# A planned two-layer kernel: VectorE work recorded one instruction at a time, and a plan that weighs what waits behind a task

## The chip, the cores and the metric

The kernel runs on one core of a Trainium2 chip. A core has a matmul engine (TensorE, PE in the profile, with its weight loads as PEld), a vector engine (VectorE, DVE), an engine for activation functions (ScalarE, ACT), a general engine (GpSimd, POOL) and SyncE (SP), which issues most DMAs here. Each engine works through its own queue in order; semaphores tie the queues together. The metric is the device time of one execution, in microseconds (us). A profile is one execution taken with the hardware profiler.

## The reference, cut to what matters

An input of 16 x 256 tokens of 128 features goes through four stages, each with a residual and a normalisation without weights:

```python
    x = _layernorm(x + _L0_attn_ref(x, ...), axis=-1)   # 16 heads of 64, softmax over 256 keys
    x = _layernorm(x + _L0_ffn_ref(x, ...), axis=-1)    # token routed to one of 64 spline tiles
    x = _layernorm(x + _L1_attn_ref(x, ...), axis=-1)   # linear attention and a window of 65, gated
    x = _layernorm(x + _L1_ffn_ref(x, ...), axis=-1)    # causal attention, then 8 experts
```

The last one is the longest:

```python
        h = layernorm(x, ln_g, ln_b)
        q = l2norm((h @ Wq) per head) * q_scale
        k = l2norm((h @ Wk) per head) * k_scale
        logits = q @ k.T * QK_SCALE, masked to the causal half
        out = (softmax(logits) @ v) @ Wo
        h = layernorm(out, ln_g, ln_b)
        gate = softmax(h @ gate_w + gate_b)
        hid = gelu(h @ w1[e] + b1[e])
        moe = sum over e of gate[e] * (hid @ w2[e] + b2[e])
        return layernorm(moe, ln_g, ln_b)
```

All eight experts are computed for every token. Everything is float32.

## The kernel before, in words

**Tiling.** The 4,096 tokens form 8 groups (`NG`) of 512, four tiles (`NJ`, index `j`) of 128 tokens on partitions. Each group goes through five stages, functions `stage_a` (attention of layer 0), `stage_b` (routing to spline tiles), `stage_c` (linear and window attention), `stage_d` (causal attention) and `stage_e` (experts). A group's activations stay in one buffer `x` in SBUF; five groups have one at a time.

**Recording and planning.** The stages do not issue instructions. They call `W.add(engine, cost, function, r=, w=)`, which records a task: the engine that may run it (a letter; "VS" lets the planner choose VectorE or ScalarE), a cost in ns, the objects it reads and writes, and `at`, a due place on a common scale (group number plus stage number plus a fraction). `add` derives from reads and writes which tasks wait for which. Buffers are taken from classes of slots (`SLOTS`): a task that first touches a buffer needs a free slot.

`Plan.order` (L144) then builds the whole order at once. It keeps a clock per engine, and repeatedly takes, over all engines, the task that could start earliest, ties going to the smaller `at`. A start takes in the ends of its forerunners plus `LAG` of their engine (`OWN` if it is the same engine), the free slots, 1,300 ns (`SWITCH`) for a change of the ScalarE table, and 93 ns (`DRAIN`) for a change of matmul tile shape (`mode`). A gelu of the experts carries a `burst`: ScalarE, once it has begun a burst (two experts, eight gelus), runs nothing else until the burst is done. The resulting order is issued as it is; each engine's queue is fixed by it.

**Places that the change touches.**

- `pair` (L577) does one pair of heads of stages a and d: `scores` into a two-bank PSUM tile `s` (there are two such tiles), `top` (in d: add the causal mask L607, two maxima L612, a product L614; in a: one maximum L616), per head `weigh` on ScalarE (exp, L634), a reciprocal (L641), `norm` on POOL (L647), a transposition on PE (L662), a copy (L529 on ACT, L531 on DVE) and `values`.
- `layernorm` (L533): `stats` (four statistics L540 and four aggregates L542), `root` on POOL (L545, L549) and `scaled` (L553), each one task for all four tiles.
- `affine` (L922): gamma, beta and residual as three POOL operations over 512 columns (L927).
- `rsqrt` (L1146): one task of 12 small VectorE steps, each reading the one before, L1152 to L1160.
- Window attention in `stage_c` (L935): masked queries `qm` made on POOL (L1031), `top` (L1064, L1065), `divide` (L1109, L1110).
- `stage_e` (L1320): both weights of an expert in one slot `we` (two slots); `up` matmuls into gelu (L1346), `down` matmuls per tile `j`, and one task `gated` of four multiply-adds into `moe` (L1361); after the last expert `layernorm`, `affine`, `layernorm` and the output DMA (L1368).
- All matmuls through the helper `mm` have line L523.

Of the kernel before, what the change touches and what calls it, by code (L numbers as in the profile page):

```python
# [46 lines left out]
    ("ov", 256, 8),  # L47
    ("m", 64, 26),
    ("k1", 256, 4),
    ("b", 512, 2),  # L50
    ("sc", 288, 1),
    ("c", 512, 8),
    ("qm", 512, 2),
    ("pbC", 512, 2),
# [5 lines left out]
    ("e", 512, 1),  # L60
    ("hid", 512, 5),
    ("we", 1024, 2),
# [20 lines left out]

class Plan:

    LAG = {"P": 270.0, "V": 150.0, "S": 170.0, "G": 120.0, "Q": 0.0, "D": 0.0}
    OWN = 80.0
    SWITCH = 1300.0  # L90
    DRAIN = 93.0

# [8 lines left out]
    def add(self, eng, cost, fn, r=(), w=(), at=None, table=None, burst=None, mode="f", hold=()):  # L101
# [9 lines left out]
        for objs, writes in ((r, False), (w, True)):  # L111
            for o in objs:
                o, part = o if isinstance(o, tuple) else (o, None)
                if isinstance(o, Buf):
                    bufs[id(o)] = o
                for q, (writers, readers) in self.state.setdefault(id(o), {}).items():
                    if part is None or q is None or q == part:
                        before.update(writers)
                        if writes:
                            before.update(readers)  # L120
# [23 lines left out]
    def order(self):  # L144
        free = {e: 0.0 for e in "PVSGQD"}
# [17 lines left out]
        while done < len(self.tasks):  # L163
            best = None
            avail = {c: sorted(x for x in v if x is not None) for c, v in slots.items()}
            for e, ts in cand.items():
                pick = None
                for t in ts:
# [3 lines left out]
                    for x, end in t.ready.items():  # L172
                        start = max(start, end + (self.OWN if x == e else self.LAG[x]))
# [65 lines left out]
def kernel(ctx: ExitStack, tc: tile.TileContext, a: dict, out: bass.AP):  # L239
# [293 lines left out]
    def layernorm(o, z, name, after=()):  # L533

        mv, rs = W.buf("m", "mv" + name), W.buf("m", "rs" + name)

        def stats():
            st = mv()[:, 8 : 8 + NJ * 6].rearrange("p (j s) -> p j s", s=6)
            for j in range(NJ):
                nc.vector.bn_stats(st[:, j, :], z(J, d=D)[:, j, :])  # L540
            for j in range(NJ):
                nc.vector.bn_aggr(mv()[:, 2 * j : 2 * j + 2], st[:, j, :])  # L542

        def root():
            nc.gpsimd.tensor_scalar(  # L545
                rs()[:, NJ : 2 * NJ], mv()[:, 0 : 2 * NJ].rearrange("p (j s) -> p j s", s=2)[:, :, 1], EPS, 1.0,
                ALU.add, ALU.mult,
            )
            nc.gpsimd.tensor_tensor(out=rs()[:, 0:NJ], in0=rs()[:, NJ : 2 * NJ], in1=mhalf, op=ALU.pow)  # L549

        def scaled():
            for j in range(NJ):
                nc.vector.tensor_scalar(  # L553
                    o(J, d=D)[:, j, :], z(J, d=D)[:, j, :], mv()[:, 2 * j : 2 * j + 1], rs()[:, j : j + 1],
                    ALU.subtract, ALU.mult,
                )

        W.add("V", NJ * (195 + 70), stats, r=[z, *after], w=[mv])
        W.add("G", 1300, root, r=[mv], w=[rs])
        W.add("V", NJ * 257, scaled, r=[z, mv, rs], w=[o])  # L560

# [15 lines left out]
    def pair(pi, qT, kT, v, ov, causal, rq, un=0):  # L577
# [24 lines left out]
        def top():  # L602
            s = sps(S2, a=2)
            n = nmx(n=4, pattern="p (a b) -> p a b", a=2)
            if causal:
                diag = s[:, :, P : 3 * P].rearrange("p a (b k) -> p a b k", k=P)
                nc.vector.tensor_tensor(  # L607
                    out=diag, in0=diag, in1=cmask.unsqueeze(1).unsqueeze(1).to_broadcast([P, 2, 2, P]), op=ALU.add
                )
                for qc in range(2):  # L610
                    c0, nk = col[qc]
                    nc.vector.tensor_reduce(n[:, :, qc], s[:, :, c0 : c0 + nk], AX.X, ALU.max, negate=True)  # L612
                rqp = rq("p (b i m) -> p i m b", n=16, b=2, i=2)[:, pi, 2 * un : 2 * un + 2, :]
                nc.vector.tensor_tensor(out=n, in0=n, in1=rqp, op=ALU.mult)  # L614
            else:
                nc.vector.tensor_reduce(n, s.rearrange("p a (b k) -> p a b k", k=S), AX.X, ALU.max, negate=True)  # L616

        cost = 1790 if causal else dve(1024)
        W.add("V", cost, top, r=[rq] if causal else [], w=[sps, nmx])
# [207 lines left out]
    def stage_b(g):  # L827
# [82 lines left out]
        def add_up():  # L910
            for q, j in enumerate(order):
                V.scalar_tensor_tensor(
                    y(J, d=D)[:, j, :], pv()[:, q, 65:NPAR], mag()[:, q : q + 1], xx(J, d=D)[:, j, :], ALU.mult, ALU.add
                )

        W.add("V", 4 * 259, add_up, r=[pp, mag, xx], w=[y, end_b])
# [5 lines left out]
    def affine(y, gam, bet, xx):  # L922

        nJ = [P, NJ, D]
# [10 lines left out]
    def stage_c(g):  # L935
# [48 lines left out]
        for b in range(2):  # L984
# [24 lines left out]
            def divide(b=b, pn2=pn2, rden=rden):  # L1009
                r = rden()[:, :2]  # L1010
                V.tensor_scalar(r, pn2()[:, :, D], 1e-6, None, ALU.add)
                V.reciprocal(r, r)
                V.tensor_tensor(
                    out=lin(J, d=D)[:, 2 * b : 2 * b + 2, :], in0=pn2()[:, :, :D],
                    in1=r.unsqueeze(2).to_broadcast([P, 2, D]), op=ALU.mult,
                )

            W.add("V", 360 + dve(256), divide, r=[pn], w=[rden, (lin, b)])
# [3 lines left out]
            for i, (w0, w1_) in enumerate(win_of):  # L1022
# [39 lines left out]
                def top(sps=sps, nmx=nmx, nk=nk, t0=t0):  # L1062
                    s8 = sps("p (u k) -> p u k", u=8)[:, :, :nk]
                    V.tensor_tensor(out=s8, in0=s8, in1=band[:, :, t0 : t0 + nk], op=ALU.add)  # L1064
                    V.tensor_reduce(nmx()[:, :8], s8, AX.X, ALU.max, negate=True)  # L1065

                W.add("V", 130 + 2 * dve(8 * nk), top, w=[sps, nmx])
# [40 lines left out]
                def divide(po=po, rw=rw, c0=c0):  # L1108
                    V.reciprocal(rw()[:, :QC], po()[:, QC : 2 * QC])  # L1109
                    V.tensor_tensor(out=winT()[:, c0 : c0 + QC], in0=po()[:, :QC], in1=rw()[:, :QC], op=ALU.mult)  # L1110

                W.add("V", 700, divide, r=[po], w=[rw, (winT, (b, i))])
# [33 lines left out]
    def rsqrt(o, x, n, eps):  # L1146

        ve, y, u = W.buf("m", "ve"), W.buf("m", "y"), W.buf("m", "u")

        def go():  # L1150
            V = nc.vector
            V.tensor_scalar(ve(n=n), x(n=n), eps, None, ALU.add)  # L1152
            yi = y(n=n).bitcast(I32)
            V.tensor_scalar(yi, ve(n=n).bitcast(I32), 1, None, ALU.logical_shift_right)
            V.tensor_scalar(yi, yi, -1.0, float(0x5F3759DF), ALU.mult, ALU.add)
            for k in range(3):
                src, dst = (y, o) if k % 2 == 0 else (o, y)
                V.tensor_mul(u(n=n), src(n=n), src(n=n))
                V.scalar_tensor_tensor(u(n=n), u(n=n), -0.5, ve(n=n), ALU.mult, ALU.mult)
                V.scalar_tensor_tensor(dst(n=n), u(n=n), 1.5, src(n=n), ALU.add, ALU.mult)  # L1160

        W.add("V", 2465 + 12 * (n - 16), go, r=[x], w=[ve, y, u, o])

    def stage_d(g):
# [9 lines left out]
        def half(b, hf):  # L1174
# [13 lines left out]
            for u in range(2):  # L1188
# [12 lines left out]
                def keep(e, ps_q=ps_q, qT=qT, u=u):  # L1201
                    for i in range(2):
# [7 lines left out]
                W.add("VS", (782, 714), keep, r=[ps_q], w=[qT])  # L1210
# [109 lines left out]
    def stage_e(g):  # L1320
# [4 lines left out]
        n = NJ * NE  # L1325
        tg, gT, pb2, moe = W.buf("p", "tg"), W.buf("k1", "gT"), W.buf("p", "pb2"), W.buf("e", "moe")
# [3 lines left out]
        W.add("VS", (dve(512), scl(512)), lambda e: copy(e, moe(), pb2()), r=[pb2], w=[moe])  # L1330
        for e_ in range(NE):
            W.at = base + e_ / NE
            burst = (g, e_ // NBURST)
            we = W.buf("we", "we")

            def fetch(e_=e_, we=we):
                nc.sync.dma_start(out=we()[:, :512], in_=a["L1_ffn_w1"][e_])
                nc.sync.dma_start(out=we()[:, 512:].rearrange("p (c d) -> p c d", d=D), in_=a["L1_ffn_w2"][e_].rearrange("(c p) d -> p c d", p=P))

            W.add("Q", 5000, fetch, w=[we], at=W.at - 0.2)  # L1340
            pe_, hids = W.buf("p", "pe"), []
            for c in range(NFC):
                ph, hid = W.buf("p", "phE"), W.buf("hid", "hid")
                W.add("P", pe(512), lambda ph=ph, we=we, c=c: mm(ph(), we()[:, c * P : (c + 1) * P], h2()), r=[we, h2], w=[ph, chain_e], burst=burst, hold=[hid])
# [3 lines left out]
            for j in range(NJ):  # L1348
                def down(j=j, pe_=pe_, we=we, hids=hids):
                    for c in range(NFC):  # L1350
                        mm(
                            pe_()[:, j * P : (j + 1) * P], hids[c]()[:, j * P : (j + 1) * P], we()[:, 512 + c * D : 512 + (c + 1) * D],
# [3 lines left out]
                W.add("P", pe(P, count=NFC), down, r=[we] + hids, w=[(pe_, j)])  # L1356

            def gated(e_=e_, pe_=pe_):
                for j in range(NJ):
# [3 lines left out]
            W.add("V", 4 * 259, gated, r=[pe_, gate], w=[moe])  # L1363
        W.at = base + 1.0
        layernorm(moe, moe, "E1")
        affine(moe, lngb, lnbb, xx)
        layernorm(xx, moe, "E2")
        W.add("Q", 2500, lambda: nc.sync.dma_start(out=y_out[g], in_=xx(J, d=D)), r=[xx])  # L1368
# [47 lines left out]
```

## Time and profile before

| | |
|---|---|
| median of 3 runs | 2226.43 us (2225.33 to 2226.8) |
| the profiled execution's own time | 2226.4 us |
| its span, first to last instruction | 2224.7 us |
| mean granted TensorE clock | 0.986 |
| last matmul ends | 2208.76 us |
| ScalarE table loads | 59, 1283 ns each |

In a row of groups stand: line, engine, operation, tile written and tiles read (buffer numbers left out), shapes, count | busy time of all, mean ns of one | idle time of the engine just before them and what ended it. A row of waits names the waiting engine and line, what it waited for, and total, times and longest in us. "Busy" of an engine is the union of its instructions; ends of matmuls are modelled.

| engine | busy us | share of the span |
|---|---|---|
| PEld | 1563.7 | 70% |
| DVE | 1663.4 | 75% |
| ACT | 1308.8 | 59% |
| POOL | 784.0 | 35% |

### The profile page before, as it was taken

The numbers are of one execution on the slowest core, as the hardware profiler recorded it, in microseconds if no ns is written. First come the engines' busy times: TensorE is split into PE (matmuls) and PEld (weight loads), VectorE is DVE, ScalarE is ACT, GpSimd is POOL, SyncE is SP. The second block draws the span as 40 slices with busy tenths as digits, with TensorE's granted clock in tenths as the row PEclk, the third lists the DMA queues.
The fourth block names the chain that finished last, engine by engine and source line by source line (L and its number), as shares of the span: only waits on it lengthen the run. The fifth ranks groups of instructions, "written<-read, shape, count | busy, mean of one in ns | idle before, by whom it ended". The sixth has DMA issues, their size and how long they took to land.

```text
span 2224.7 us, 49747 instructions
## 1 busy us (share of the span) xinstructions
PE 2099.0 (94%) x18506; PEld 1563.7 (70%) x18506; DVE 1663.4 (75%) x4784; ACT 1308.8 (59%) x3817; POOL 784.0 (35%) x1413
## 2 busy tenths in 40 slices
PE   8999999999999998999999999999899989989987
PEld 6777777767767766776777767777667667766655
DVE  5788899886688965788757895788856984784742
ACT  4566666764667643676647664666545755654632
POOL 3444362452143621435304360243502530431311
PEclk9999999999999999999999999999999999999998
DMA  5100000000100001000010001100011001101101
GB/s 141 30 1 2 2 1 2 2 2 26 48 15 2 2 29 35 25 2 1 23 41 25 2 1 40 39 6 2 2 43 34 7 2 55 27 1 44 39 20 43
DMA packets 69490, 47.98 MB, mean 22 GB/s; under 512 B 12064, under 2 KB 59904, under 8 KB 69248
## 3 DMA queue, kind: packets, MB, share of 16 engines
q1 hardware_dynamic: 68672, 43.74, 7.3%
q8 instruction: 147, 2.41, 0.5%
q10 hardware_dynamic: 576, 1.05, 0.2%
q14 instruction: 95, 0.78, 0.1%
HBM read 41.89 MB, written 2.88 MB: 20 GB/s over the span
## 4 chain that ended last, share of the span: by engine, by line
PE 53%; DVE 20%; ACT 5%; POOL 2%; issue 2%; POOLq 0%; DVEq 0%; ACTq 0%
PE p L523 39%; PE s L523 6%; PE p L662 4%; DVE m L612 2%; ACT pb L634 2%; PE p L1082 2%; DVE s L607 2%; DVE m L540 1%; DVE m L616 1%; POOL pb L647 1%; DVE x L553 1%; DVE m L614 1%; PE p L1265 1%; DVE uq L1208 1%; DVE s L1064 1%
## 5 line engine op out<-in xcount | busy, mean ns | idle before, releaser
L647 POOL TENSOR_SCALAR pb<-pb,m 128x256 f32<-128x256 f32 (+1 forms) x1024 | 453.8, 460 | 766.9 <-DVE m L641 675.1
L1346 ACT ACTIVATE hid<-p,b 128x512 f32<-128x512 f32 x256 | 170.5, 688 | 304.7 <-PE p L523 290.4
L662 PE MATMUL p<-ident,pb 128*128 128x128 f32 x1792 | 290.0, 282 | 14.1 <-POOL pb L647 5.0
L634 ACT ACTIVATE pb<-s,m,m 128x128 f32<-128x128 f32 (+1 forms) x512 | 257.4, 522 | 61.5 <-DVE m L614 50.7
L634 ACT ACTIVATE pb<-s,m 128x256 f32<-128x256 f32 x512 | 238.8, 490 | 70.5 <-DVE m L616 59.4
L662 PEld LDWEIGHTS p<-ident,pb 128*128 128x128 f32 x1792 | 206.1, 142 | 102.0 <-POOL pb L647 46.8
L523 PE MATMUL p<-h,we 128*128 128x512 f32 x512 | 264.2, 617 | 9.5 <-ACT hid L1346 4.9
L523 PEld LDWEIGHTS p<-we,hid 128*128 128x128 f32 x2048 | 243.3, 194 | 29.9 <-issue 15.7
L523 PE MATMUL p<-we,hid 128*128 128x128 f32 x2048 | 252.8, 279 | 3.9 <-ACT hid L1346 2.1
L529 ACT COPY pt<-p 128x512 f32<-128x512 f32 (+1 forms) x316 | 168.6, 540 | 129.1 <-PE p L662 117.3
L1361 DVE SCALAR_TENSOR_TENSOR e<-p,m,e 128x128 f32<-128x128 f32 x256 | 71.9, 344 | 143.7 <-PE p L523 122.0
L616 DVE TENSOR_REDUCE m<-s 128x4 f32<-128x1024 f32 x128 | 154.7, 1217 | 15.7 <-PE s L523 14.5
L1255 POOL TENSOR_TENSOR kn<-kn,m 128x512 f32<-128x512 f32 x64 | 66.2, 1049 | 283.9 <-DVE m L1160 232.3
L1076 ACT ACTIVATE pbC<-s,m 128x96 f32<-128x96 f32 (+1 forms) x512 | 135.3, 382 | 33.8 <-DVE m L1065 29.3
L523 PE MATMUL s<-ua,ua 64*128 64x256 f32 x1024 | 139.4, 395 | 10.5 <-ACT pb L634 9.0
L523 PE MATMUL s<-ud,uq 64*128 64x128 f32 (+1 forms) x1024 | 118.0, 352 | 21.4 <-ACT pb L634 20.4
L523 PE MATMUL p<-pt,ua 128*64 128x256 f32 x1024 | 136.2, 388 | 1.7 <-ACT pt L529 1.3
L531 DVE COPY pt<-p 128x512 f32<-128x512 f32 (+1 forms) x196 | 120.9, 621 | 20.9 <-PE p L662 19.5
L612 DVE TENSOR_REDUCE m<-s 128x2 f32<-128x256 f32 (+1 forms) x256 | 130.8, 553 | 5.3
L523 PEld LDWEIGHTS p<-h,we 128*128 128x128 f32 x512 | 84.9, 193 | 64.4 <-issue 30.6
L1031 POOL TENSOR_TENSOR qm<-c,hm 128x512 f32<-128x512 f32 x64 | 68.1, 1070 | 153.4 <-PE s L523 132.8
L523 PEld LDWEIGHTS s<-ua,ua 64*128 64x128 f32 x1024 | 91.2, 187 | 39.5 <-ACT pb L634 14.3
(273 smaller groups left out, 4294.0 us busy)
## 6 DMA issues: line engine op xcount, KB each, us to landing
we<-in_L_ffn_w_dram SPq DMA_DIRECT2D x128, 256.0 KB, 2.8
x<-_attn_hidden_states_dram SPq DMA_DIRECT2D x8, 256.0 KB, 2.8
out_dram<-x SPq DMA_DIRECT2D x8, 256.0 KB, 2.3
dpad<-k SPq DMA_DIRECT2D x1, 768.0 KB, 10.3
wq<-in_L_attn_Wq_dram ACTq DMA_DIRECT2D x2, 256.0 KB
wkv<-in_L_attn_Wkv_dram ACTq DMA_DIRECT2D x2, 256.0 KB, 6.8
wkv<-in_L_attn_Wkv_dram SPq DMA_DIRECT2D x2, 256.0 KB, 5.6
wo<-in_L_attn_Wo_dram SPq DMA_DIRECT2D x1, 512.0 KB, 8.4
```

What stands on the lines that cost most here:

```text
L523: nc.tensor.matmul(o, lhsT=lhsT, rhs=rhs, start=start, stop=stop)
L529: nc.scalar.copy(o, i)
L531: nc.vector.tensor_copy(o, i)
L612: nc.vector.tensor_reduce(n[:, :, qc], s[:, :, c0 : c0 + nk], AX.X, ALU.max, negate=True)
L616: nc.vector.tensor_reduce(n, s.rearrange("p a (b k) -> p a b k", k=S), AX.X, ALU.max, negate=True)
L634: act(pb()[:, c0 : c0 + nk], s[:, par, c0 : c0 + nk], AF.Exp, bias=nmx()[:, 2 * par + qc : 2 * par + qc + 1], accum_out=sums()[:, 2 * par ...
L647: eng.tensor_scalar(pb()[:, c0 : c0 + nk], pb()[:, c0 : c0 + nk], sums()[:, 2 * par + qc : 2 * par + qc + 1], 1.0, ALU.mult, ALU.mult,)
L662: nc.tensor.transpose(tps()[:, at * P : (at + 1) * P], pb()[:, c0 + kc * P : c0 + (kc + 1) * P], ident)
L1031: (V if e == "V" else G).tensor_tensor(out=qm("p (h q) -> p h q", q=QC), in0=qw()[:, c0 : c0 + QC].unsqueeze(1).to_broadcast(nq), in1=hm8. ...
L1076: act(pb("p (u k) -> p u k", u=4)[:, u, :nk], s8[:, hp, :nk], AF.Exp, bias=nmx()[:, hp : hp + 1])
L1346: W.add("S", 571, lambda ph=ph, hid=hid, ec=ec: act(hid(), ph(), AF.Gelu_apprx_tanh, bias=b1[:, ec : ec + 1]), r=[ph], w=[hid], table="gel ...
L1361: V.scalar_tensor_tensor(m, pe_()[:, j * D : (j + 1) * D], gate()[:, j * NE + e_ : j * NE + e_ + 1], m, ALU.mult, ALU.add)
```

## The change

Tasks on VectorE that held several instructions become one task per instruction: `layernorm`'s statistics, aggregates and scaling, `top` and `divide` of the attentions, `add_up` in stage b, `rsqrt`, `gated`. Parts of an object can now be named by a kind and a number (`("j", j)`), and `overlap` decides whether two parts conflict: parts of different kinds do, different parts of the same kind do not.

The planner gets other lags, an `OWN` per engine, and a new outer loop: `rest` of a task is its cost plus the longest chain of tasks behind it; the due place becomes `at - rest / weight`; ten weights are planned, and the order whose planned end is earliest is issued. The weight that results here is 4e4.

An expert's weights lie in two slots of their own classes (`w1`, `w2`), loaded by two tasks. `begun` lets the expert matmuls start only when `moe` has been set. The last group's norms, affine and output run tile by tile, with the affine on VectorE and its result kept in `moe`. Slot counts change.

```diff
-    ("ov", 256, 8),
-    ("m", 64, 26),
-    ("k1", 256, 4),
+    ("ov", 256, 7),
+    ("m", 64, 30),
+    ("k1", 256, 5),
...
-    ("c", 512, 8),
-    ("qm", 512, 2),
-    ("pbC", 512, 2),
+    ("c", 512, 7),
+    ("qm", 512, 1),
+    ("pbC", 512, 3),
...
-    ("e", 512, 1),
-    ("hid", 512, 5),
-    ("we", 1024, 2),
+    ("e", 512, 2),
+    ("hid", 512, 6),
+    ("w1", 512, 2),
+    ("w2", 512, 2),
...
-    LAG = {"P": 270.0, "V": 150.0, "S": 170.0, "G": 120.0, "Q": 0.0, "D": 0.0}
-    OWN = 80.0
+    LAG = {"P": 265.0, "V": 178.0, "S": 200.0, "G": 60.0, "Q": 0.0, "D": 0.0}
+    OWN = {"P": 0.0, "V": 130.0, "S": 80.0, "G": 80.0, "Q": 0.0, "D": 0.0}
+    RESTS = (1e5, 8e4, 6e4, 5e4, 4e4, 3e4, 2.5e4, 2e4, 1.5e4, 1e4)
...
-                    if part is None or q is None or q == part:
+                    if overlap(q, part):
...
     def order(self):
+        rest = {}
+        for t in reversed(self.tasks):
+            rest[t.seq] = min(t.cost) + max([self.LAG[t.eng[0]] + rest[n.seq] for n in t.then], default=0.0)
...
+        def again(weight):
+            for t, t.wait, at in first[0]:
+                t.ready, t.end, t.at = {}, None, at - rest[t.seq] / weight
...
+        for weight in self.RESTS:
+            line = again(weight)
+            if line is not None:
+                ends.append((max(end for _, _, _, end in line), weight))
+        return again(min(ends)[1])
...
-    def layernorm(o, z, name, after=()):
+    def layernorm(o, z, name, after=(), js=range(NJ), own=False):
+        if own:
+            for j in js:
+                layernorm(o, z, name, after, [j])
+            return
...
-        W.add("V", NJ * (195 + 70), stats, r=[z, *after], w=[mv])
-        W.add("G", 1300, root, r=[mv], w=[rs])
-        W.add("V", NJ * 257, scaled, r=[z, mv, rs], w=[o])
+        for j in js:
+            W.add("V", 195, lambda j=j: nc.vector.bn_stats(st(j), z(J, d=D)[:, j, :]), r=[*zs, *after], w=[(mv, ("j", j))])
+        for j in js:
+            W.add("V", 70, lambda j=j: nc.vector.bn_aggr(mv()[:, 2 * j : 2 * j + 2], st(j)), w=[(mv, ("j", j))])
...
+        W.add("G", 1300 if len(js) == NJ else 800, root, r=[mv], w=[rs])
...
-        W.add("V", 2465 + 12 * (n - 16), go, r=[x], w=[ve, y, u, o])
+        each = lambda fn, r, w: W.add("V", 60 + n, fn, r=r, w=w)
+        each(lambda: V.tensor_scalar(ve(n=n), x(n=n), eps, None, ALU.add), [x], [ve])
...
-            we = W.buf("we", "we")
+            w1, w2 = W.buf("w1", "w1"), W.buf("w2", "w2")
+            W.add("Q", 2500, lambda e_=e_, w1=w1: nc.sync.dma_start(out=w1(), in_=a["L1_ffn_w1"][e_]), w=[w1], at=W.at - 0.2)
...
-            W.add("V", 4 * 259, gated, r=[pe_, gate], w=[moe])
+                W.add("V", 259, gated, r=[pe_, gate], w=[(moe, ("j", j))])
...
-        layernorm(moe, moe, "E1")
-        affine(moe, lngb, lnbb, xx)
-        layernorm(xx, moe, "E2")
-        W.add("Q", 2500, lambda: nc.sync.dma_start(out=y_out[g], in_=xx(J, d=D)), r=[xx])
+        last = g == NG - 1
+        layernorm(moe, moe, "E1", own=last)
+        affine(moe, lngb, lnbb, xx, own=last)
+        if last:
+            layernorm(moe, moe, "E2", own=True)
+            for j in range(NJ):
+                W.add("Q", 2500, lambda j=j: nc.sync.dma_start(out=y_out[g][:, j, :], in_=moe(J, d=D)[:, j, :]), r=[(moe, ("j", j))])
+        else:
+            layernorm(xx, moe, "E2")
+            W.add("Q", 2500, lambda: nc.sync.dma_start(out=y_out[g], in_=xx(J, d=D)), r=[xx])
```

## The prediction

> **What bounds the kernel.** I read the busy shares first, then the waits of TensorE, then stretches of the span, then single instructions.
>
> ```profile
> span 2224.7 us, 49747 instructions
> ...
> PE 2099.0 (94%) x18506; PEld 1563.7 (70%) x18506; DVE 1663.4 (75%) x4784; ACT 1308.8 (59%) x3817; POOL 784.0 (35%) x1413
> ```
>
> TensorE is busy for 94% of the span; nothing in the change removes a matmul. A busy PE is still not a full one. At the steady start-to-start times of the trace (one pass over 512 columns 430 ns, 256 columns 216, 128 columns 111, halves and quarters where tiles run side by side), all matmul passes add up to about 1,880 us. So 2224.7 - 1880 = 345 us is loss, in five parts: the tail behind the last matmul, 15.9 (it ends at 2208.8); visible idle of PE before that, 109.8; changes of tile shape (below), 81; a granted clock of 0.986, about 29; and the rest, about 105, short delays hidden under the modelled length of the matmul before.
>
> Of the 109.8, added up over all rows of the waits by the engine waited for, ACT ended 47.8, DVE 40.6, POOL 15.8, a DMA at the start 5.6. So 104 us stand in 2,100 us of work, mostly about 1 us at a time. The largest row (total, times, longest) is scores that wait for a PSUM bank which exp still reads:
>
> ```profile
> PE s L523 <- ACT pb L634: 30.5, 27, 4.4
> ```
>
> Where they stand, by stretches (length, then busy time per engine):
>
> ```profile
> 400.00:520.00 120.00, 116.94 (x1097) 87.67 (x1096) 105.30 (x297) 81.13 (x268) 61.73 (x111) 1.00 0.01 2
> ...
> 2000.00:2080.00 80.00, 77.50 (x476) 54.36 (x477) 37.49 (x108) 36.41 (x75) 8.71 (x18) 0.98 0.16 47
> 2080.00:2150.00 70.00, 59.51 (x412) 41.07 (x411) 51.34 (x167) 43.17 (x135) 31.23 (x61) 0.93 0.05 12
> ```
>
> In the first, attention of several groups overlaps: PE idles 3 us, but DVE is 88% busy, a second bound. In the second, experts stand amid other work and DVE is only half used. In the third the last group's attention (stage d) stands alone: 10.5 us of 70 idle.
>
> **The change, part by part.** It is mostly another order of the same work, so I counted in the instruction orders of both kernels.
>
> *VectorE in single instructions.* Neighbours on DVE where the second reads what the first wrote fall from 1,079 to 308 (norm statistics, scaling and gated sums, which share only the tile's name, left out). What one costs:
>
> ```profile
> L542 DVE BATCH_NORM_AGGREGATE m<-m 128x2 f32<-128x6 f32 x288 | 26.2, 155 | 0.0
> ...
> L1158 DVE TENSOR_TENSOR m<-m 128x32 f32<-128x32 f32 x96 | 20.4, 213 | 3.4
> L1047 DVE TENSOR_TENSOR vm<-p,bvw 96x32 f32<-96x32 f32 x128 | 15.1, 177 | 2.2 <-PE p L523 2.2
> ```
>
> Busy time over count against mean length: L542 takes 155 ns each but only 91 of engine time, L1047 177 and 118; independent instructions overlap. L1158, each reading its forerunner, takes 213 of 213. In the timeline the rsqrt's steps start 225 ns apart, L1047's 97. So a dependent neighbour costs 0.13 us, and 771 fewer save 100 us of DVE. The Trainium skill says otherwise ("VectorE: DVE Perf Modes", Rules for kernel authors): chained operations drain in any case, one should lower their count, not the semaphores. The count here rises (4,784 to 4,899), so by the rule DVE loses a little. The row decides: 91 against 155 is overlap. Against the 100 stand 90 copies that move from ACT to DVE, at 0.6 us about 54. DVE falls to about 1,615.
>
> *Table loads.* 59 become 36; gelus run in 10 groups (six of 32) instead of 23.
>
> ```profile
> L1346 ACT ACT_TABLE_LOAD x23 | 29.5, 1283 | 0.4
> ```
>
> 23 x 1.283 = 29.5 us off ACT; "ScalarE: Activation LUTs" (What ACT_TABLE_LOAD costs) adds a drain, 2.66 us a switch, 61 in all. In the trace the next activation starts 1.29 us after the load, so 29.5 stands. With the copies gone ACT falls by about 80, to 1,230. Neither saving is the span's: both engines are off the bound. They count only through PE's waits.
>
> *PE's waits.* For each matmul group that reads another engine's result, I set the PE work between it and the group that feeds that engine against the length of the chain in between (start-to-start: an exp of two tiles 0.90, a 512-column copy 0.60). Groups with too little PE work in between: score transpositions 42 of 512 before, 24 after; values 41 and 21 of 256; down projections 26 and 16 of 256. The summed shortfall falls by 24%. Queueing on ACT and DVE is not in it, and improves too. Of 104 us I take 24%: **-25**; bounds 0 and -52. The 105 of hidden delays come of the same closeness, but the trace doesn't name them: half that share, **-12**; bounds 0 and -25.
>
> *Tile shapes.* Neighbouring matmuls of different shape fall from 905 to 792.
>
> ```profile
> 251.59 0.65 PE L523 MATMUL p<-ptC,vm 128*32 128x64 f32 x32
> 252.06 0.63 PE L523 MATMUL p<-ptC,hones 128*32 128x64 f32 x32
> 252.62 2.05 PE L523 MATMUL p<-wo,ov 128*128 128x128 f32 x16
> ```
>
> The same 32 passes take 0.47 before their own shape and 0.56 before another: 0.09. 113 x 0.09 = **-10**, in full, since PE is the bound.
>
> *The tail.*
>
> ```profile
> 2208.80 1.13 DVE L1361 SCALAR_TENSOR_TENSOR e<-p,m,e 128x128 f32<-128x128 f32 x4 [5.34 <-PE p L523]
> ...
> 2213.59 1.26 POOL L927 TENSOR_TENSOR e<-e,lngb 128x512 f32<-128x512 f32 x1 [1.23 <-DVE e L553]
> ...
> 2221.33 0.38 SPq L1368 DMA_DIRECT2D out_dram<-x  x1
> ```
>
> From 2208.8 to 2221.3 run gated sum, norm, three POOL operations (4.0 us from start to end), norm. After, three of four gated sums run under the last matmuls (about -0.8), and the affine moves to DVE tile by tile. But POOL now takes eight roots in a row instead of two, and DVE's order still has all four statistics ahead of the first scaling. A root of four columns takes 1.3 (0.20 and 1.01 with a gap between); of one column no row shows it: 0.6 if the power goes by columns, 1.3 if by instruction. First root at +1.4, four roots, 1.9 us of DVE, 0.8 of statistics, four roots, scaling: at 0.85 a root about +10.9 against +12.5. **-2** with three quarter-size output DMAs issued earlier; bounds -4 and +2.4.
>
> *What costs.* Group 6's experts draw together, so between them and the last expert stage stand 322 matmuls instead of 233: stage d alone for 38% longer, and 0.38 x 10.5 = **+4**. One slot for qm instead of two: in two places score groups stand 1 and 6 matmuls apart, and the second waits for POOL (1.04 us) and its handover: **+2**; zero if PE is late anyway. The split weight slots, the second moe and the sixth hid slot: no wait of PE on these loads stands in the trace, 2.8 us to land against 7.4 us per expert; cost nothing, and if that cover went, one landing per expert pair.
>
> **Sum.** The profiled execution took 2226.4 (1.7 around its span), as the median 2226.43. 2226.4 - 25 - 12 - 10 - 2 + 4 + 2 = **2183**.
>
> **Rivals.**
> *Only what is certain.* PE's waits merely move to the next late engine: then 2226.4 - 10 - 2 + 4 + 2 = 2220. For it: DVE is 88% busy amid attention and gets 90 copies more. Against: the cover grows for every kind of group.
> *Attention loses its filler (slower).* Across each group's expert stretch, other matmuls stand between: 1,675 in all before, 819 after. So 856 matmuls (856 / 10,658 x 2,100 = 170 us) lose the experts as cover, and ACT is shut to exp throughout a run of 32 gelus. If they idle as stage d alone does (15%) instead of 2%, that is +22, and the waits gain nothing: 2220 + 22 = 2242. It decides as soon as such stretches idle by more than 4% over today's (6 / 170). For it: the third stretch. Against: other groups remain as filler there, unlike at the end.
> *Waits halve*, visible and hidden, and the clock recovers with the gaps (0.93 in the third stretch): 2226.4 - 52 - 50 - 10 = 2115 to 2150.
>
> **Numbers.** Forecast as summed 0.58; only what is certain 0.17; filler lost 0.17; waits halve 0.08. A measurement here tells 0.2% (4.5 us). The likeliest case lies wholly faster; the second splits, 0.11 to faster and 0.06 to same; the third gives 0.15 slower and 0.02 same; the fourth is faster. Faster 0.77, same 0.08, slower 0.15. The range runs from part of the fourth case to the second: 2140 to 2226.
>
> **What would show it.** DVE busy near 1,615 with L1158's counterpart at less than its length in engine time; 36 table loads; PE's idle before its last matmul near 85 instead of 110, less in the row of scores waiting for exp; PE's last end 10 to 40 us earlier; about 2 us less behind it. Wrong if expert stretches are as full as now but attention beside them idles more, if DVE stays at 1,660, or if the tail grows, which would mean a root costs by instruction.

## The result, and the profile after

| | before | after |
|---|---|---|
| median (lowest to highest), us | 2225.88 (2225.03 to 2226.8) | 2197.57 (2195.72 to 2199.41) |
| profiled execution, its span | 2226.4, 2224.7 | 2198.37, 2196.6 |
| last matmul ends | 2208.8 | 2182.3 |
| idle time of PE before that | 109.8 | 103.6 |
| busy time of PE | 2099.0 | 2078.7 |
| behind the last matmul | 15.9 | 14.3 |
| ScalarE table loads | 59 | 36 |

After over before is 0.9873 (95% interval 0.9856 to 0.989): 28 us faster. The span is 28.1 shorter, and the table splits it: 6.2 of idle time of PE, 20.3 of its busy time, 1.6 of the tail. The matmuls are the same, so the busy time fell by what stands hidden in it: late starts that the modelled ends of matmuls cover, changes of tile shape above all.

The page of the kernel after, its span and its busy shares:

```profile
span 2196.6 us, 49778 instructions
...
PE 2078.7 (95%) x18506; PEld 1579.2 (72%) x18506; DVE 1640.2 (75%) x4899; ACT 1237.5 (56%) x3691; POOL 775.6 (35%) x1422
```

The waits of PE in the kernel after (line, what it waited for: total, times, longest):

```profile
PE s L559 <- ACT pb L687: 20.3, 24, 1.9
PE p L559 <- DVE pt L567: 8.0, 17, 1.3
PE p L715 <- POOL pb L700: 7.7, 11, 2.5
...
PE s L559 <- POOL qm L1092: 1.3, 1, 1.3
```

The row of scores that wait for exp fell from 30.5 to 20.3. Over all rows, waits for ACT fell from 47.8 to 35.4, but those for DVE rose from 40.6 to 45.2 and those for POOL from 15.8 to 17.2. Half of what ACT gave back, other engines took.

Where it stands, by stretches of the kernel after (start and end, length; busy time of PE, PEld, DVE, ACT and POOL; granted clock; share and GB/s of DMA):

```profile
812.00:881.00 69.00, 68.79 (x480) 50.44 (x479) 26.87 (x89) 28.44 (x46) 4.43 (x7) 1.00 0.21 58
881.30:1061.00 179.70, 174.66 (x1778) 137.51 (x1777) 163.90 (x482) 121.07 (x399) 88.81 (x163) 1.00 0.02 6
...
1645.30:1782.60 137.30, 121.69 (x1218) 88.18 (x1217) 119.61 (x406) 79.74 (x246) 59.26 (x101) 0.95 0.02 5
1851.70:1971.60 119.90, 107.35 (x1158) 79.82 (x1158) 102.59 (x323) 74.31 (x236) 49.28 (x89) 0.97 0.02 6
2036.90:2123.90 87.00, 71.58 (x522) 50.85 (x521) 66.50 (x214) 48.55 (x159) 37.44 (x76) 0.92 0.03 7
1573.30:2182.30 609.00, 562.36 (x4620) 408.08 (x4618) 365.07 (x1180) 309.24 (x816) 151.99 (x273) 0.96 0.10 28
```

The first stretch holds nearly nothing but one group's experts: PE idles 0.2 us in 69. The second is the attention of several groups, with no experts beside it: 5.0 us idle in 180, DVE 91% busy. Together they are the steady middle, and there the change wins: from the first expert matmul of group 0 to that of group 2 it takes 519 us (542.0 to 1061.0), before 551 (519.5 to 1070.4). The next three rows are the attention stretches between the last four groups' experts. Few groups are left there, and experts no longer stand between: 15.6, 12.6 and 15.4 us idle, 43.6 in all, and the clock falls to 0.92. The same three stretches before had 31.9:

```profile
1719.20:1826.70 107.50, 95.86 (x1076) 72.28 (x1074) 101.67 (x322) 69.32 (x216) 55.80 (x88) 0.97 0.02 7
1912.20:2002.20 90.00, 80.26 (x713) 58.57 (x714) 79.18 (x249) 53.86 (x167) 41.18 (x74) 1.00 0.03 7
2084.90:2146.50 61.60, 51.11 (x374) 35.93 (x374) 47.75 (x153) 36.40 (x125) 31.23 (x61) 0.95 0.03 10
```

The idle share is nearly the same, 12% of 259 us before and 13% of 344 after; the stretches are longer. So from the start of group 4's experts to the last matmul the kernel after needs 609.0 us (its last row above), and the same part took 603.7 before, with somewhat more matmuls in it:

```profile
1605.10:2208.80 603.70, 561.73 (x4706) 407.58 (x4705) 393.53 (x1215) 334.15 (x861) 158.91 (x279) 0.98 0.10 29
```

Matmul passes at the prediction's steady start-to-start times are 488 of the 609 and 495 of the 603.7. The loss, the length less these passes, rose there from 109 to 121.

VectorE and ScalarE, groups of the kernel after, and last the kernel before's L614, the counterpart of L664 (busy, mean ns | idle before):

```profile
L583 DVE BATCH_NORM_AGGREGATE m<-m 128x2 f32<-128x6 f32 x288 | 27.3, 151 | 0.0
L664 DVE TENSOR_TENSOR m<-m,m 128x4 f32<-128x4 f32 x128 | 23.4, 183 | 0.2
L1224 DVE TENSOR_TENSOR m<-m 128x32 f32<-128x32 f32 x96 | 21.0, 219 | 0.8
L1414 ACT ACT_TABLE_LOAD x10 | 12.8, 1283 | 0.2
...
L614 DVE TENSOR_TENSOR m<-m,m 128x4 f32<-128x4 f32 x128 | 31.1, 243 | 4.4
```

L664 is the product after the two maxima. Before it took 243 ns each, with 4.4 us idle ahead of it; now other work stands between, and it is 183. The gelus load their table 10 times, not 23. DVE fell by 23.2 us, though the copies of the helper on it (L531, after L567) rose from 675 to 765, by 53 us of busy time, and the last group's affine adds 12 operations. So the rest of its work takes some 80 us less; that this is the standing apart follows from the rows above and was not tried alone.

### The profile page after: what moved, and what is told of

Read it like the earlier page. It is cut to its first block, busy times and chain, and to the rows that moved or that the text cites. A ratio compares the mean times of both kernels' runs of the same rounds, so it can differ in the third digit from the quotient of the medians.

```text
span 2196.6 us, 49778 instructions
## 1 busy us (share of the span) xinstructions
PE 2078.7 (95%) x18506; PEld 1579.2 (72%) x18506; DVE 1640.2 (75%) x4899; ACT 1237.5 (56%) x3691; POOL 775.6 (35%) x1422
## 5 line engine op out<-in xcount | busy, mean ns | idle before, releaser
L715 PE MATMUL p<-ident,pb 128*128 128x128 f32 x1792 | 274.0, 282 | 17.8 <-POOL pb L700 7.7
L715 PEld LDWEIGHTS p<-ident,pb 128*128 128x128 f32 x1792 | 201.6, 142 | 89.7 <-POOL pb L700 48.1
L559 PEld LDWEIGHTS p<-w,hid 128*128 128x128 f32 x2048 | 238.5, 192 | 24.4 <-issue 17.5
L559 PE MATMUL p<-h,w 128*128 128x512 f32 x512 | 243.3, 611 | 4.6 <-ACT hid L1414 3.1
L559 PE MATMUL p<-w,hid 128*128 128x128 f32 x2048 | 243.5, 276 | 1.3 <-DVE c L1074 0.5
L567 DVE COPY pt<-p 128x512 f32<-128x512 f32 (+1 forms) x274 | 169.0, 621 | 32.2 <-PE p L715 28.6
L559 PEld LDWEIGHTS p<-h,w 128*128 128x128 f32 x512 | 92.7, 194 | 104.9 <-issue 77.4
L565 ACT COPY pt<-p 128x384 f32<-128x384 f32 (+1 forms) x238 | 123.1, 534 | 69.8 <-PE p L715 57.1
L658 DVE TENSOR_REDUCE m<-s 128x2 f32<-128x512 f32 (+1 forms) x256 | 133.0, 546 | 0.7
L559 PE MATMUL p<-pt,ud 128*64 128x256 f32 (+1 forms) x1024 | 112.8, 338 | 3.4 <-DVE pt L567 2.9
```

Source lines behind the costliest of these rows:

```text
L559: nc.tensor.matmul(o, lhsT=lhsT, rhs=rhs, start=start, stop=stop)
L565: nc.scalar.copy(o, i)
L567: nc.vector.tensor_copy(o, i)
L658: lambda qc=qc, c0=c0, nk=nk: nc.vector.tensor_reduce(nm()[:, :, qc], sps(S2, a=2)[:, :, c0 : c0 + nk], AX.X, ALU.max, negate=True),
L715: nc.tensor.transpose(tps()[:, at * P : (at + 1) * P], pb()[:, c0 + kc * P : c0 + (kc + 1) * P], ident)
```

## The experiments

The theories are named by letters in some expectations. A: the weight of what waits behind a task pays alone, by drawing each group's experts together. B: the single VectorE instructions pay alone. C: it takes both. D: what pays is the drawn-together expert stretch itself, with its fewer table loads. "Over before" is each kernel's ratio to the kernel before on the same chip, with its 95% interval. PE's idle time is that before its last matmul. An edit of slots, lags or tasks makes the planner try its weights again, and another may win: 4e4 in the kernel after, in others as told. The planned end is the planner's own time for the last task of an order, summed from the costs in the kernel's text.

### One part alone

**no_rest**: the single tasks without the weight.

```diff
-    RESTS = (1e5, 8e4, 6e4, 5e4, 4e4, 3e4, 2.5e4, 2e4, 1.5e4, 1e4)
+    RESTS = (1e12,)
```

> The changed kernel with the single weight 1e12, so that what waits behind a task counts for nothing; single VectorE instructions, slots and the tail stay. Theory A (the order of the stages is what gains: expert stretches drawn together, attention of several groups overlapped): without the weight the gain goes, 2215 to 2245 us. Theory B (single VectorE instructions shorten the waits wherever they stand): most of the gain stays, 2195 to 2208 us.

2271.61 us (2270.64 to 2273.66), 1.0209 (1.0194 to 1.0224): 46 us slower than before. Its row of scores waiting for exp:

```profile
PE s L559 <- ACT pb L687: 42.4, 37, 2.7
```

PE's idle time is 141.5, its shape changes 902. B falls. So does the picture of the cause that A and D share: the experts are drawn together here too (560 us from first to last expert matmul over all groups, after 585, before 767), with 40 table loads, and the loss lies in the attention between, 351 us against 277 after.

**rest_alone**: the kernel before, its lumps and lags, with the weight loop. With its own slot counts none of the ten weights gives a complete order (the planner runs out of slots), so it has those of the kernel after, except that an expert's weights stay in one slot.

```diff
+        for weight in self.RESTS:
+            line = again(weight)
...
-    ("c", 512, 8),
-    ("qm", 512, 2),
-    ("pbC", 512, 2),
+    ("c", 512, 7),
+    ("qm", 512, 1),
+    ("pbC", 512, 3),
...
```

> The kernel before, with the weighing of the work behind a task and the changed slot counts (an expert's weights still in one slot), VectorE tasks in lumps and lags as before. Theory A in its narrow form (the weight alone makes the order): 2195 to 2210 us. Theory C (weight and single instructions only work together, since lumps hold up the chains that the weight wants first): 2215 to 2240 us.

2231.36 us (2229.14 to 2233.59), 1.0028 (1.0016 to 1.004): no gain. Idle 122.4, DVE 1692.6, 65 table loads, 801 shape changes. The weight lowers the changes of shape without the single tasks, but not the waits. Neither half pays alone, so C stands, though each run is one order and orders differ (below). The planned ends say the same over more orders: 2123.3 before; five complete orders of rest_alone, none earlier than 2126.5; nine of the kernel after, none later than 2119.5. The `begun` mark and the tail by tiles were not taken out alone.

### Slots and lags

**old_slots**: the kernel after with the slot counts of before (`w1`, `w2` keep two each).

```diff
-    ("qm", 512, 1),
-    ("hid", 512, 6),
+    ("qm", 512, 2),
+    ("hid", 512, 5),
...
```

> The changed kernel with the slot counts of before (the weights still in separate slots). If the slot counts are a detail: within 10 us of the changed kernel, 2195 to 2208 us. If the order lives from them (one qm less, one hid and one moe more): 2215 us or more.

2191.54 us (2188.35 to 2194.25), 0.9847 (0.9833 to 0.9862), with the weight 3e4.

**one_weight_slot**: the kernel after with both weights of an expert in one slot `we`.

```diff
-    ("w1", 512, 2),
-    ("w2", 512, 2),
+    ("we", 1024, 2),
...
```

> The changed kernel with both weights of an expert in one slot again (two slots, one loading task). In its order the experts spread among other work as before (58 table loads instead of 36). Theory D (what gains is the drawn-together expert stretch: 32 us of loss in it instead of 81, and 23 table loads less on ScalarE): most of the gain goes, 2215 us or more. Theory C (weight and single instructions together pack the work, and where the experts stand hardly matters): 2190 to 2204 us, the loss moving from the attention stretches back to the expert stretches.

2195.1 us (2190.33 to 2197.27), 0.9861 (0.9845 to 0.9877), with the weight 3e4. The time is that of the kernel after, with another picture: 58 table loads instead of 36, and the experts spread out again (680 us from first to last). So the gain needs neither fewer loads nor drawn-together experts, and D falls.

**old_lags**: the kernel after with `LAG` and `OWN` of before.

```diff
-    LAG = {"P": 265.0, "V": 178.0, "S": 200.0, "G": 60.0, "Q": 0.0, "D": 0.0}
-    OWN = {"P": 0.0, "V": 130.0, "S": 80.0, "G": 80.0, "Q": 0.0, "D": 0.0}
+    LAG = {"P": 270.0, "V": 150.0, "S": 170.0, "G": 120.0, "Q": 0.0, "D": 0.0}
+    OWN = {"P": 80.0, "V": 80.0, "S": 80.0, "G": 80.0, "Q": 0.0, "D": 0.0}
```

> The changed kernel with the lags and the equal OWN of 80 of before. If single instructions and the weight carry the gain: 2190 to 2205 us. If the planner needs the new lags (130 ns on VectorE behind its own result) to place them: 2210 us or more.

2193.88 us (2192.32 to 2194.95), 0.9855 (0.9834 to 0.9875), with the weight 2.5e4. All three medians lie 2 to 6 us below the kernel after, with overlapping intervals, and each has another order throughout. None of slots, weight slots and lags carries the gain.

### How much hangs on which weight is taken

**weight_3e4** and **weight_1e5**: the kernel after with one weight only.

```diff
-    RESTS = (1e5, 8e4, 6e4, 5e4, 4e4, 3e4, 2.5e4, 2e4, 1.5e4, 1e4)
+    RESTS = (3e4,)
```

> The changed kernel with the one weight 3e4, the next to the chosen 4e4. If the gain belongs to weighing as such: 2195 to 2205 us. If it hangs on the pick among the ten orders: 2210 us or more.

2231.54 us (2229.08 to 2240.62), 1.0037 (1.0021 to 1.0053): slower than before, with everything of the change in it but a neighbouring weight.

> The changed kernel with the one weight 1e5, where what waits behind a task counts least of the ten. If the gain belongs to weighing as such: under 2215 us. If it hangs on the pick among the ten orders: 2215 us or more.

2220.31 us (2215.11 to 2223.65), 0.9972 (0.996 to 0.9984). The expert stretches of group 0 and group 3 with the weight 3e4:

```profile
537.00:639.00 102.00, 90.94 (x605) 63.31 (x604) 38.26 (x119) 34.54 (x59) 4.07 (x8) 0.90 0.14 40
1357.00:1457.00 100.00, 88.44 (x607) 61.71 (x606) 38.84 (x122) 34.37 (x60) 3.88 (x7) 0.93 0.15 40
```

and the same two in the kernel after, weight 4e4:

```profile
542.00:633.00 91.00, 87.74 (x666) 64.99 (x666) 47.23 (x145) 38.37 (x82) 7.74 (x13) 1.00 0.16 44
1331.00:1400.00 69.00, 68.89 (x485) 50.70 (x481) 27.07 (x89) 28.73 (x46) 4.72 (x8) 1.00 0.20 58
```

Drawn-together experts are not full by themselves: with 3e4 PE idles 11 us in each, and the clock falls to 0.90. With 1e5 the expert stretches are well filled, and the attention loses 305 us. Between three weights the same code spreads over 34 us, more than the gain, so the gain belongs to weighing together with the pick.

The pick is not blind. Planned ends are 2094.6 for 4e4, 2113.6 for 3e4 and 2114.9 for 1e5, and the three kernels above that picked among ten orders, with other winners, run at 2191 to 2195 us. But a planned end is no measurement: 3e4 was planned 9.7 us ahead of the kernel before and ran 6.5 behind it. The planner knows nothing of the clock, which withholds 44.4 us there and 32.4 in the kernel after (over its length up to the last matmul, each time at half clock counted half).

### The price of a change of tile shape

**shape_same** adds one matmul of 128 rows by 128 columns ahead of each of the 256 up projections, into the same PSUM tile, which the projection then overwrites. **shape_half** adds the same with 64 rows: the same passes in the same order, but another tile shape than its neighbours. Of the line, the changed part, in shape_half:

```diff
-lambda ph=ph, w1=w1, c=c: mm(ph(), w1()[:, c * P : (c + 1) * P], h2())
+lambda ph=ph, w1=w1, c=c: (mm(ph()[:, :P], w1()[0:64, c * P : (c + 1) * P], h2()[0:64, :P]), mm(ph(), w1()[:, c * P : (c + 1) * P], h2()))
```

> The changed kernel with one more matmul of 128 columns and all 128 rows ahead of each of the experts' 256 matmuls into gelu, in the same PSUM tile, overwritten by the matmul behind it. Two passes of 0.11 us each: 57 us more than the changed kernel if PE is the bound there, about 2254 us.

> As shape_same, but the added matmul takes 64 rows, so that 512 changes of tile shape are added. If a change costs 0.09 us in the run time, as read from two starts in the trace: 46 us more than shape_same. If the drain is hidden by waits that are there anyway: under 15 us more.

2247.71 us (2244.39 to 2251.04; 1.0101, 1.0077 to 1.0124) and 2344.03 (2343.83 to 2344.22; 1.0534, 1.0513 to 1.0555). shape_same costs 50 us, of the 57 expected; for shape_half both expectations miss. All engines have the same instructions in the same order in both. The shape changes are 792 and 1,262, 470 more and not 512: 96.3 us for 470 is **0.205 us each**, twice the prediction's 0.09. The timeline of shape_half, last experts (start, length; each first row is four extra matmuls and four projections, two passes each):

```profile
2292.26 5.95 PE L559 MATMUL p<-h,w 64*128 64x128 f32 x16
2298.05 3.73 PE L559 MATMUL p<-w,hid 128*128 128x128 f32 x32
```

and of shape_same:

```profile
2204.34 4.49 PE L559 MATMUL p<-h,w 128*128 128x128 f32 x16
2208.67 3.73 PE L559 MATMUL p<-w,hid 128*128 128x128 f32 x32
```

From the first start to the next row's, 5.79 against 4.33: 1.46 for eight changes, with the first half of the first one ahead of the first start. In single starts the price has two halves: the first pass of the new shape comes 0.09 late, and the second another 0.10 late (0.215 behind the first where 0.11 is the rule for 128 columns, 0.53 where 0.43 is for 512). The prediction read the length up to the first start only, and the planner's `DRAIN` of 93 ns is that first half too. The second half stood in the trace of before too, in the row after the three that it showed:

```profile
254.51 1.03 PE L523 MATMUL p<-wkv,xT 128*128 128x256 f32 x4
```

From 252.62 to 254.51 are 1.89 us for 16 passes of 0.112, which is 1.79: 0.10 more, behind the first. By single starts in that trace the second half is not always so long: 0.05 where a transposition or a tile of 64 columns follows, 0.02 for 32 columns. The Trainium skill ("TensorEngine Tiling (Array Packing)", Key Properties) states that a change of tiling mode drains TensorE, and gives no figure; for a change between 128 and 64 rows, 0.205 us is one.

### Filler for the last attention stretches

**fill_7**: the experts of group 6 are held back, two by two, until pairs 1, 5, 9 and 13 of the last group's stage d are through, so that they stand among its attention. **fill_567**: the same for the experts of groups 4, 5 and 6. **fill_all**: for groups 0 to 6. A held group's `stage_e` is recorded behind the next group's `stage_d`, and each pair there sets a mark that the up projections read (fill_567; of the last line the changed part):

```diff
+        W.add("VS", (dve(256), scl(256)), lambda e: copy(e, ov(), ops()[:, :S]), r=[ops], w=[ov] + ([mark] if mark is not None else []))
...
+            gate_on = [marks[g + 1][[1, 1, 5, 5, 9, 9, 13, 13][e_]]] if g + 1 in (5, 6, 7) else []
...
-r=[w1, h2, begun]
+r=[w1, h2, begun] + gate_on
```

> The changed kernel, with group 6's experts held back: each pair of them may begin only when pairs 1, 5, 9, 13 of the last group's causal attention have been copied out, so that they fill it. Theory A with the end as its weak place (attention without expert work beside it idles there: 15 us of 87): 8 to 14 us under the changed kernel, 2184 to 2190 us, and the stretch between the last two expert stages gone. Theory B: no change or slower by the added table loads, 2196 to 2202 us.

2191.01 us (2190.55 to 2191.56), 0.9846 (0.983 to 0.9862), weight 2e4: 6.6 us under the kernel after, a little less than expected, and no more than the old slots brought (2191.54).

> As fill_7, with the experts of groups 4, 5 and 6 held back into the causal attention of groups 5, 6 and 7. If the idle of attention at the end is what the changed kernel leaves lying: 8 to 20 us under fill_7, 2171 to 2183 us. If fill_7 only drew another order by luck (its stretch gains were less than expected): 2188 to 2200 us.

2158.12 us (2153.07 to 2160.91), **0.9693 (0.9673 to 0.9713)**, weight 2.5e4: below both kernels, and below what was expected. The page, and the stretch from group 4's first expert to the last matmul:

```profile
span 2157.5 us, 49711 instructions
...
PE 2059.6 (95%) x18506; PEld 1566.2 (73%) x18506; DVE 1657.6 (77%) x4937; ACT 1236.2 (57%) x3670; POOL 782.0 (36%) x1422
```

```profile
1601.50:2142.80 541.30, 513.71 (x4265) 380.94 (x4257) 359.22 (x1140) 288.40 (x738) 149.00 (x264) 0.98 0.11 32
```

The 541.3 us hold 467 of passes: a loss of 75 against 121 in the kernel after, 46 less. The whole execution is 39 faster. So the gain lies where the edit put it. The weight differs too, and no run holds it fixed; but the planned ends of fill_567 lie under those of the kernel after at each of the nine weights that both complete (by 2 to 46 us; 2064.6 against 2094.6 for the picks). PE's idle time is 83.1, its waits for ACT 23.5 instead of 35.4; table loads rose to 53, and the time that the clock withholds fell from 32.4 to 13.7 us.

> As fill_567, with every group's experts held back into the causal attention of the next group. If expert work is worth having as filler everywhere: under fill_567, 2145 to 2158 us. If it is worth it only where no other group's attention stands beside (the end), and costs table loads elsewhere: 2158 to 2180 us, with the same last stretches.

2193.28 us (2183.76 to 2199.34), 0.985 (0.9819 to 0.9882), weight 4e4. Both expectations miss.

```profile
PE 2074.0 (95%) x18506; PEld 1581.9 (72%) x18506; DVE 1699.5 (78%) x5003; ACT 1242.5 (57%) x3625; POOL 786.4 (36%) x1422
```

DVE works 59 us longer than in the kernel after, there are 74 table loads, and the clock is 0.980, withholding 37.5 us where fill_567 has 13.7. In the steady middle other groups already were filler. By the planned ends, 2073.3 against 2064.6, the edit there costs 9 us; what makes it 35 on the chip stays open, with the clock's 24 us as the largest difference on show.

## Why the prediction was right, and which terms were not

The direction and the range hold; the forecast of 2183 was 14.6 us too low. The mechanism holds in part. A closer order did shorten PE's time, but the waits that were to bring 25 of the 43 us brought few, and some 20 of the 28 measured (an estimate, below) come from the smaller number of shape changes, at twice the price taken. Fewer changes alone do not make the gain: rest_alone and the weight 3e4, with 801 each, save 18 us of busy time at full clock too, and lose it again, 13 and 7 us to idle time and 10 and 19 to the clock. That the forecast still came near is partly luck. Step by step:

- **PE's waits, -25: the term that failed.** With the +4 and +2 set against it, PE's idle time was to fall by 19; it fell by 6.2, to 103.6 where the sign set was 85. By engine: the 24% of cover was taken off all waits alike. Those for ACT did shrink so, by 12.4 of 47.8, 26%, but those for DVE grew by 4.6 and for POOL by 1.4. That the waits would move to DVE, 88% busy and with 90 copies more, was the first rival's argument. The copies themselves explain little of it: waits for the copying helper rose by 1.6 of the 4.6 (from 13.3 to 14.9). What else made DVE late was not tried alone.
- **Attention alone, +4: mis-sized.** The same 13 us by place: only the matmuls ahead of the last expert stage were counted, not the two stretches before. The three last attention stretches idle 12 us longer, at nearly the same share of a greater length, so everything else fell by 18. This is the second rival's mechanism, true at the end and not in the middle, where other groups fill.
- **Tile shapes, -10.** The count was right, the price about half of what it is. Not all changes cost 0.205: priced by what follows each, from single starts of the trace of before, and the first half only where PE did not wait there, those of the whole order come to about 146 us before and 126 after, an estimate of -20.
- **Hidden delays, -12.** PE's busy time fell by 20.3 while the clock withheld 6.8 us more (25.6 before, 32.4 after, up to the last matmul). So 27 went at full clock, and beside the shapes' 20 this leaves about -7. It is a remainder, not a measurement. The pool of 105 that the term was a share of was mostly something else: by the same prices some 64 of it are the second halves of shape changes.
- **The clock** was not in the sum: +7. By length and clock of their rows, the three last attention stretches lose 17 us to it, where the same three lost 7 before.
- **The tail, -2**: -1.6. The place was off. No gated sum ran under the last matmuls, since each still reads the whole PSUM tile of its expert (`r=[pe_, gate]`), but the root of one column took what was taken for it.

The timeline of the tail of the kernel after:

```profile
2182.36 1.13 DVE L1430 SCALAR_TENSOR_TENSOR e<-p,m,e 128x128 f32<-128x128 f32 x4 [4.54 <-issue]
...
2184.44 0.19 POOL L587 TENSOR_SCALAR m<-m 128x1 f32<-128x1 f32 x1 [69.26 <-DVE m L583]
2184.72 0.55 POOL L591 TENSOR_TENSOR m<-m,mhalf 128x1 f32<-128x1 f32 x1
2185.30 0.35 DVE L597 TENSOR_SCALAR e<-e,m,m 128x128 f32<-128x128 f32 x1 [0.75 <-POOL m L591]
...
2191.52 3.03 SPq L1441 DMA_DIRECT2D out_dram<-e  x4
...
2193.84 0.35 DVE L597 TENSOR_SCALAR e<-e,m,m 128x128 f32<-128x128 f32 x1 [0.56 <-POOL m L591]
```

A root is 0.28 from start to start and then 0.55, 0.83 in all (0.85 was taken). The last scaling ends 11.9 us behind the last matmul (+10.9 was expected, +12.5 was before).

- **qm, +2**: its row of waits shows 1.3.
- **VectorE and ScalarE.** 36 loads and ACT at 1237.5 came as worked out (1,230); DVE at 1640 missed its 1,615 by 25. The sign set for L1158's counterpart, less engine time than length, did not come: L1224 has 219 of 219, since its steps do not stand beside each other, and a group's busy time does not show what of other groups overlaps it. L664 shows the saving instead. The row was right against the rule on chained operations: DVE's count rose by 115 and its busy time fell by 23.2.

The errors partly cancel: the forecast took 13 us too much off for idle time and 5 for hidden delays and left out 7 for the clock, and took 10 too little off for shapes. Nor did any step weigh that one order of ten was taken: 3e4 has nearly as few shape changes (801) and is slower than before. The planned ends, 2123.3 and 2094.6, differ by 28.8 us, close to the 28.3 measured; run less planned end is 103 us in both, but from 89 to 122 in the other kernels here that add no matmul, so such closeness is not the rule.

## What to carry to other kernels

Counts and closeness in an order tell the direction, but with a planner that builds the order task by task, the pick of one order among near ones is worth as much as the change (34 us between three weights here). So read the planner's own end first, then run several of the best and choose by the measured time. Work that is taken off engines which do not bound counts only through the bound engine's waits, and those can move to the next late engine: sum them by engine, and look at the last stretches on their own, where less work is left to fill. Keep work that depends on little, here the experts, for the wind-down (2158.12 us against 2197.57).

## What the runs showed of the hardware

A change between tiles of 128 and 64 rows costs PE about 0.2 us (96.3 us for 470), half of it as a late second pass, which the first start behind the change does not show.

The granted clock follows the gaps of PE, even where these are under 1 us each. In the rows above it is 0.98 to 1.00 where PE is busy for 96% or more, but 0.90 to 1.00 at 88 to 90%, so the busy share alone does not set it. In the stretch of the weight 3e4 with 0.90 it lies at half for 17 us on end, among gaps of 0.6 to 0.8 us:

```profile
578.60:595.60 17.00, 12.98 (x40) 9.58 (x41) 3.51 (x9) 0.00 (x0) 0.00 (x0) 0.50 0.00 0
```

The Trainium skill ("TensorE: Matmul & The Clock Gate", The HAM clock gate) has the clock set by how busy TensorE has been recently, which agrees. A wait can thus be paid twice. In the kernel after, behind a wait of 2.45 us, 16 passes of 128 columns take 3.07 us to the next row's start, where 1.79 is the rule:

```profile
1546.65 3.27 PE L559 MATMUL p<-fo,ov 128*128 128x128 f32 x16
1549.72 0.96 PE L611 MATMUL p<-ident,d 128*128 128x128 f32 x4
```

fill_567 has a clock of 0.991 over its span, the kernel after 0.983.

A power on POOL takes 0.55 us for one column and, in the trace of before, 1.01 for four: part goes by instruction, part by column.
